# Squaring a hidden-state row on GpSimd from SBUF instead of reloading it for ScalarE: the row norms of a GRU with a mixture-of-experts stage

## The chip, the cores and the metric

The kernel runs on one core of a Trainium2 chip. The metric is the device time of one execution, in microseconds (us). The time before is the median of three runs. The profile is one further execution, recorded by the hardware profiler.

## The reference, cut to what matters

A GRU runs over 256 time steps for 16 batch rows with 512 features. Its hidden states, 4096 tokens of 512 features, then pass a mixture of eight low-rank experts of which each token uses two. The router divides a token by its norm before it multiplies by `router_w`, so every token needs the sum of its squared features.

```python
def cell(h, x):
    gi = x @ W_ih + b_ih
    gh = h @ W_hh + b_hh
    i_r, i_z, i_n = jnp.split(gi, 3, axis=-1)
    h_r, h_z, h_n = jnp.split(gh, 3, axis=-1)
    r = jax.nn.sigmoid(i_r + h_r)
    z = jax.nn.sigmoid(i_z + h_z)
    n = jnp.tanh(i_n + r * h_n)
    h_new = (1.0 - z) * n + z * h
    return (h_new, h_new)

norm = jnp.maximum(jnp.linalg.norm(x, axis=-1, keepdims=True), 1e-12)
router_logits = x / norm @ router_w
routing_weights = jax.nn.softmax(router_logits.astype(jnp.float32), axis=-1)
rw, selected_experts = jax.lax.top_k(routing_weights, TOP_K)
rw = rw / jnp.sum(rw, axis=-1, keepdims=True)
combine = jnp.sum(jax.nn.one_hot(selected_experts, N_EXPERTS, dtype=rw.dtype) * rw[..., None], axis=1)
for e in range(N_EXPERTS):
    out = out + combine[:, e, None] * (x @ Wa[e] @ Wb[e])
x = x + out
```

Everything is float32.

## The kernel before

The steps of the recurrence are written out one by one, in 32 blocks of eight (`TS = 8`); in this text t is a step's place in its block, 0 to 7. A step (`step`) has a fixed chain. PE multiplies the transposed hidden state by the recurrent weights, 16 matmuls for the r and n gates (`into_rn`, L921), then 16 for the z gate (`into_z`, L931). ACT takes the tanh for r (L947), z (L952) and n (L956). DVE forms the candidate in two instructions that read PSUM (L954, L955), then `zh` (L959), `m` (L961) and `rows` (L963), which each read two tensors in SBUF, and transposes the result into `hist` (L966). That last transpose releases the next step's matmuls. A second transpose (`back`, L974) makes the next step's row form of h.

Behind this chain the program places other work. PE multiplies the next steps' inputs (`gate_in`, L269 and L277) after each step's own matmuls. Agents bring the rest: `Early` prepares some inputs' products ahead, `Route` routes the tokens of one block, `Chunk` sorts routed tokens into expert slots in DRAM, `Slab` runs one expert on 128 slots, `Combine` gathers the two results of a token and adds them, and `Moe` handles the last three blocks without sorting. The first 29 blocks go by the sorted way, in chunks of 7, 11, 7 and 4 blocks. Every agent has a list of `Piece`s, each with a least distance in steps (`gap`), a planned matmul cost and the room in buffers that it takes. `choose` picks pieces for each step; `advance(0, ...)` issues their matmuls after the step's own, and `advance(1, ...)` issues the rest behind the step's chain. The order on every engine is then fixed by `keep_order`: each engine executes strictly in the order in which the program was written.

GpSimd (POOL) has this work in the loop: copies of a slab's weights (`wag` L677 and `wbg` L681), which wait for an earlier slab's matmuls to free a buffer; the `Early` bias additions (L391 to L393); the square root of a norm (L629, a power of one half); small operations of the top-2 (L307, L637); and the indirect DMAs that scatter tokens (L558) and gather results (L750).

A block's `Route` starts in the block after it. In t = 0 `keep` writes the 128 rows of h to DRAM (`H`, eight DMAs, L604), since the scatter needs them there. In t = 1 PE computes the router's logits from `hist` (L341), `fetch` issues a DMA on SP's queue that reads the rows back as `ht`, 128 tokens by 512 features (L612), and DVE transposes the logits (L622). In t = 3 `norm` squares `ht` on ACT with a running sum (L627), and POOL takes the root. In t = 4 and t = 5 follow the softmax and the top-2. The chunk itself reads the rows once more, as `ht2` (L552), when it scatters them; that stays as it is. The DMA list of the page counts both reloads under `ht<-H`, 58 in all, 29 of each.

Of the kernel before, what the change touches and what calls it, by code (L numbers as in the profile page):

```python
# [8 lines left out]
FP = mybir.dt.float32  # L9
# [7 lines left out]
AF = mybir.ActivationFunctionType  # L17
ALU = mybir.AluOpType
# [3 lines left out]
P = 128  # L22
TS = 8
# [21 lines left out]
def gru_moe_kernel(  # L45
# [47 lines left out]
    pe, dve, act, pool, sp = nc.tensor, nc.vector, nc.scalar, nc.gpsimd, nc.sync  # L93
    B, T, D = x.shape
    E, _, R = wa.shape
    NJ = D // P
    NQ = P // 32
# [18 lines left out]
    moe = ctx.enter_context(tc.tile_pool(name="moe", bufs=2))  # L116
# [29 lines left out]
    for side, src in enumerate((b_ih, b_hh)):  # L146
        for g in (0, 2, 1):
            tag = ("xg", "wbg")[side]
# [22 lines left out]
    ones = const.tile([P, 1], FP, name="ones")  # L171
    pool.memset(ones, 1.0)
    half = const.tile([P, 1], FP, name="half")
# [37 lines left out]
    rt = ps_r.tile([P, 512], FP, name="rt")  # L211
    pe.matmul(rt, lhsT=zero[:, 0:P], rhs=zero, start=True, stop=True)
    banks = []
    for n in range(2):
        pair = []
        for what in ("rn", "z"):
            g = ps_g.tile([P, 512], FP, name=f"{what}_{n}")
            for j in range(NJ):
                pe.matmul(
                    g[32 * j : 32 * j + 32, :], lhsT=zero[:, 0:32], rhs=zero,  # L220
                    start=True, stop=True,
# [5 lines left out]
    for n, parts in enumerate((((0, 0), (1, 0)), ((1, 2),), ((0, 2),), ((0, 1), (1, 1)))):  # L227
        for k, (side, g) in enumerate(parts):
            for j in range(NJ):
                pe.matmul(  # L230
                    bias_ps[32 * j : 32 * j + 32, n * P : (n + 1) * P],
                    lhsT=ones_sq[0:1, 0:32],
                    rhs=b_rows[side, g][:, j * P : (j + 1) * P],
                    start=(k == 0), stop=(k == len(parts) - 1),
# [102 lines left out]
    def router(h):  # L337

        for q in range(NQ):
            for c in range(NJ):  # L340
                pe.matmul(  # L341
                    rt[32 * c : 32 * c + E, 0:32].rearrange("p (b t) -> p b t", t=TS),
                    lhsT=wr_sb[:, q, :], rhs=tokens(h, q, c),
                    start=(q == 0), stop=(q == NQ - 1),
                )

    class Early:
# [57 lines left out]
        def plan(self):  # L405
            pieces = [
                Piece(then=[("load",)], takes="early"),
                Piece(gap=2, then=[("turn",)], takes="at"),
            ] + [
                Piece(gap=0, cost=c, pe=[("into", what, q)])  # L410
                for what, c in (("rn", 0.43), ("z", 0.22))
                for q in range(NQ)
            ] + [Piece(then=[("store",)], gives="early")]
            pieces[2].gap, pieces[2].takes = 1, ["ps"]
            pieces[9].then, pieces[9].gives = [("keep",)], ["ps", "at"]
            return pieces
# [19 lines left out]
    class Chunk:  # L436
# [113 lines left out]
        def fetch(self, k):  # L550
            ht = moe.tile([P, D], FP, tag="ht2", bufs=2, name=f"ht2_{self.c}_{k}")
            sp.dma_start(ht, self.rows[k].rearrange("b t d -> (b t) d"))  # L552
            self.ht = getattr(self, "ht", {})
            self.ht[k] = ht
# [37 lines left out]
    class Route:  # L592
# [14 lines left out]
                    )  # L607
            self.chunk.rows.append(hd)

        def fetch(self):  # L610
            self.ht = moe.tile([P, D], FP, tag="ht", name=f"ht_{self.i}")
            sp.dma_start(  # L612
                self.ht, self.chunk.rows[self.k].rearrange("b t d -> (b t) d")
            )

        def logits(self):
            router(self.hist)

        def soft0(self):

            self.lg = moe.tile([P, 32], FP, tag="lgs", name=f"lg_{self.i}")
            dve.transpose(self.lg, rt[:, 0:32])  # L622

        def norm(self):
            i = self.i
            ss = moe.tile([P, 1], FP, tag="ss", name=f"ss_{i}")
            act.activation(self.ht, self.ht, AF.Square, accum_out=ss)  # L627
            self.nrm = moe.tile([P, 1], FP, tag="nrm", name=f"nrm_{i}")
            pool.tensor_tensor(self.nrm, ss, half, ALU.pow)  # L629

        def soft1(self):
            self.ex, self.sm = softmax(self.i, self.lg, self.nrm)
# [5 lines left out]

        def plan(self):
            return [  # L640
                Piece(then=[("keep",)]),
                Piece(cost=0.35, pe=[("logits",)], then=[("fetch",), ("soft0",)]),
                Piece(gap=2, then=[("norm",)]),
                Piece(then=[("soft1",)]),
                Piece(then=[("soft2",)]),
            ]
# [466 lines left out]
    for i in range(NB):  # L1113
        rows, rows_next = rows_next, None
        for t in range(TS):
# [8 lines left out]
            elif m + 1 < T // 2:  # L1124
                q = 0 if t % 2 == 0 else 2
# [72 lines left out]
```

## Time and profile before

| | before |
|---|---|
| median of three runs | 1357.65 us (1355.23 to 1357.68) |
| the profiled execution | 1356.92 us |
| its span, first to last instruction | 1355.1 us, granted TensorE clock 0.994 |
| PE matmul busy | 1292.5 us (95%), 30378 matmuls |
| DVE, ACT, POOL busy | 736.2 us, 392.1 us, 284.4 us |
| moved by DMA | 158.67 MB |
| reload `ht<-H`, of the two kinds together | 58 of 256 KB |

The engines run beside one another, so their busy times are not to be added. A busy PE is a PE with a matmul in its pipeline; it is not a PE without room. Where in the step an engine's work falls is told by the timeline, which lists instructions in order of time with the idle time before each and what ended it.

### The profile page before, as it was taken

How to read it: one execution, taken by the hardware profiler on the slowest of the kernel's cores; microseconds unless marked ns; L12 is line 12 of the kernel's file. 1: busy time of each engine (PE TensorE's matmuls, PEld its weight loads, DVE VectorE, ACT ScalarE, POOL GpSimd, SP SyncE). 2: the span in 40 equal slices, each digit the busy share in tenths (PEclk: the TensorE clock that was granted, in tenths of full speed). 3: DMA queues.
4: the chain of work that ended last, by engine and by line, in shares of the span. 5: the costliest groups of instructions: out<-in, count | busy, mean ns of one | idle time of the engine just before them, and what ended most of it. 6: DMA issues, size and time to landing. Idle time of an engine off the chain costs nothing. (4 is left out here: it accounts for less than half of the span.)

```text
span 1355.1 us, 68450 instructions
## 1 busy us (share of the span) xinstructions
PE 1292.5 (95%) x30378; PEld 929.7 (69%) x30378; DVE 736.2 (54%) x2678; ACT 392.1 (29%) x1354; POOL 284.4 (21%) x504
## 2 busy tenths in 40 slices
PE   6899999999999999999999999999998999989996
PEld 3577777776677777777776677777766787768752
DVE  1455555555455555555555456555565555665543
ACT  1223222322233333233332233333332333323220
POOL 2000000102221000000003323221133033353452
PEclk8999999999999999999999999999999999999998
DMA  8532322223322111122124535553345345664685
GB/s 200 143 122 97 99 91 90 91 61 130 95 72 61 55 56 56 41 59 57 50 65 132 182 90 158 151 148 101 95 142 167 103 135 168 174 199 129 199 253 167
DMA packets 149477, 158.67 MB, mean 117 GB/s; under 512 B 22646, under 2 KB 103606, under 8 KB 149180
## 3 DMA queue, kind: packets, MB, share of 16 engines
q1 hardware_dynamic: 139760, 123.83, 31.1%
q0 software_dynamic: 9280, 30.42, 7.1%
q8 instruction: 238, 3.90, 1.2%
q14 instruction: 59, 0.48, 0.1%
q10 hardware_dynamic: 140, 0.05, 0.0%
HBM read 84.21 MB, written 69.99 MB: 114 GB/s over the span
## 5 line engine op out<-in xcount | busy, mean ns | idle before, releaser
L921 PE MATMUL rn<-whh,hist 128*32 128x256 f32 x8160 | 507.8, 381 | 19.9 <-DVE hist L966 14.1
L921 PEld LDWEIGHTS rn<-whh,hist 128*32 128x32 f32 x8160 | 264.0, 109 | 198.5 <-DVE hist L966 48.3
L269 PE MATMUL rn<-wih,xT 128*32 128x256 f32 x3712 | 307.3, 382 | 9.3 <-DMA wih<-in_L_cond_W_ih_dram 5.5
L931 PE MATMUL z<-whh,hist 128*32 128x128 f32 x8160 | 289.9, 273 | 6.4 <-issue 5.8
L954 DVE SCALAR_TENSOR_TENSOR n<-r,rn 128x128 f32<-128x128 f32 x256 | 73.5, 287 | 397.6 <-ACT r L947 393.0
L931 PEld LDWEIGHTS z<-whh,hist 128*32 128x32 f32 x8160 | 247.3, 110 | 51.7 <-issue 13.5
L277 PE MATMUL z<-wih,xT 128*32 128x128 f32 x3712 | 209.0, 274 | 5.5 <-ACT z L952 3.3
L947 ACT ACTIVATE r<-rn 128x128 f32<-128x128 f32 x256 | 70.9, 277 | 460.7 <-PE rn L921 448.8
L277 PEld LDWEIGHTS z<-wih,xT 128*32 128x32 f32 x3712 | 138.5, 110 | 77.3 <-issue 6.3
L269 PEld LDWEIGHTS rn<-wih,xT 128*32 128x32 f32 x3712 | 126.7, 110 | 19.0 <-issue 13.1
L959 DVE SCALAR_TENSOR_TENSOR zh<-z,h 128x128 f32<-128x128 f32 x255 | 77.8, 305 | 86.0 <-ACT z L952 83.1
L952 ACT ACTIVATE z<-z 128x128 f32<-128x128 f32 x256 | 71.0, 277 | 170.7 <-PE z L931 144.7
L698 PE MATMUL at_ps<-xgT,wag 128*32 128x128 f32 x2752 | 110.1, 273 | 3.9 <-issue 3.5
L629 POOL TENSOR_TENSOR nrm<-ss,half 128x1 f32<-128x1 f32 x29 | 16.2, 559 | 435.5 <-ACT ht L627 408.2
L713 PE MATMUL y_ps<-wbg,at 128*32 128x256 f32 x1376 | 103.2, 380 | 1.0 <-issue 0.9
L698 PEld LDWEIGHTS at_ps<-xgT,wag 128*32 128x32 f32 x2752 | 87.6, 110 | 13.9 <-issue 10.2
L966 DVE STREAM_TRANSPOSE hist<-rows 128x128 f32<-128x128 f32 x256 | 79.7, 311 | 8.7
L974 DVE STREAM_TRANSPOSE h<-hist 128x128 f32<-128x128 f32 x256 | 79.7, 311 | 8.7
L681 POOL COPY wbg<-wb_sb 128x512 f32 x86 | 56.3, 655 | 126.0 <-PE y_ps L713 125.9
L963 DVE SCALAR_TENSOR_TENSOR rows<-zh,m 128x128 f32<-128x128 f32 x256 | 75.9, 297 | 8.9
L721 ACT COPY y<-y_ps 128x512 f32<-128x512 f32 x86 | 50.1, 583 | 101.9 <-PE y_ps L713 88.3
L961 DVE SCALAR_TENSOR_TENSOR m<-z,n 128x128 f32<-128x128 f32 x256 | 77.7, 303 | 2.4 <-ACT n L956 1.4
(136 smaller groups left out, 1072.4 us busy)
## 6 DMA issues: line engine op xcount, KB each, us to landing
xg<-x_slots SPq DMA_DIRECT2D x344, 64.0 KB
y_slots<-y SPq DMA_DIRECT2D x86, 256.0 KB
ht<-H SPq DMA_DIRECT2D x58, 256.0 KB
x_slots<-zero SPq DMA_DIRECT2D x50, 256.0 KB
x<-in_x_dram SPq DMA_DIRECT2D x256, 32.0 KB
xr<-in_x_dram SPq DMA_DIRECT2D x32, 256.0 KB
out_dram<-xr SPq DMA_DIRECT2D x32, 256.0 KB
H<-rows SPq DMA_DIRECT2D x232, 32.0 KB
```

Of the source, the lines that this page charges most:

```text
L269: pe.matmul(rn[32 * j : 32 * j + 32, 0 : 3 * P].rearrange("p (g d) -> p g d", g=3)[:, 0:3:2, :], lhsT=xts[m][:, q, :], rhs=w[:, 0:3:2, j, ...
L277: ins = pe.matmul(zb[32 * j : 32 * j + 32, 0:P], lhsT=xts[m][:, q, :], rhs=w[:, 1, j, :], start=False, stop=(q == NQ - 1), skip_group_chec ...
L698: pe.matmul(self.ps[c32, 0:P], lhsT=self.wa[:, q, c32], rhs=self.xt[:, q, :], start=(q == 0), stop=(q == NQ - 1),)
L713: pe.matmul(self.ps[c32, half], lhsT=self.at[:, c32], rhs=self.wb[:, half], start=True, stop=True,)
L921: pe.matmul(rn[32 * j : 32 * j + 32, 0 : 2 * P].rearrange("p (g d) -> p g d", g=2), lhsT=hT[:, q, :], rhs=w(q, j)[:, 0:3:2, :], start=Fals ...
L931: pe.matmul(zb[32 * j : 32 * j + 32, 0:P], lhsT=hT[:, q, :], rhs=w(q, j)[:, 1, :], start=False, stop=(q == NQ - 1), skip_group_check=True,)
L954: dve.scalar_tensor_tensor(n, r, 1.0, rn[:, P : 2 * P], ALU.add, ALU.mult)
L959: dve.scalar_tensor_tensor(zh, z, 1.0, hrow, ALU.add, ALU.mult)
L961: dve.scalar_tensor_tensor(m, z, 1.0, n, ALU.subtract, ALU.mult)
L963: dve.scalar_tensor_tensor(hn, zh, 0.5, m, ALU.mult, ALU.subtract)
L966: dve.transpose(hist[:, t, :, lo : lo + 32], hn.rearrange("p (q c) -> p q c", q=NQ))
L974: dve.transpose(hrow.rearrange("p (q c) -> p q c", q=NQ), hT)
```

## The change

The norm no longer comes from reloaded rows. `fetch` and `norm` are gone from `Route`, and with them the DMA of the rows back into SBUF and ACT's squaring pass. In t = 0, with `keep`, a new `square` works on `hist` itself, which has the features on the partitions: POOL squares it quarter by quarter into a tile `sq` of 128 by 512, reading `hist` with a step so that the tokens come out in order, and adds the quarters up in two more instructions, to 128 by 128. In t = 3 four small matmuls with a column of ones (`sums`) add `sq` over the partitions into columns 32 to 63 of the router's PSUM bank. One DVE transpose of 64 columns then brings logits and sums together; it stands in t = 3 where the transpose of 32 columns stood in t = 1. POOL's root follows it. `sq` uses the two buffers that `ht` had.

```diff
-        def fetch(self):
-            self.ht = moe.tile([P, D], FP, tag="ht", name=f"ht_{self.i}")
-            sp.dma_start(
-                self.ht, self.chunk.rows[self.k].rearrange("b t d -> (b t) d")
-            )
+        def square(self):
+
+            sq = moe.tile([P, NQ, P], FP, tag="ht", name=f"sq_{self.i}")
+            for q in range(NQ):
+                h = self.hist[:, :, q, 16:32].rearrange("p t b -> p b t")
+                pool.tensor_mul(
+                    sq[:, q, :].rearrange("p (b t) -> p b t", t=TS), h, h
+                )
+            pool.tensor_add(sq[:, 0:2, :], sq[:, 0:2, :], sq[:, 2:4, :])
+            pool.tensor_add(sq[:, 0, :], sq[:, 0, :], sq[:, 1, :])
+            self.sq = sq
...
+        def sums(self):
+            for c in range(NJ):
+                pe.matmul(
+                    rt[32 * c : 32 * c + 1, 32:64],
+                    lhsT=ones, rhs=self.sq[:, 0, 32 * c : 32 * c + 32],
+                    start=True, stop=True,
+                )
+
         def soft0(self):
-            self.lg = moe.tile([P, 32], FP, tag="lgs", name=f"lg_{self.i}")
-            dve.transpose(self.lg, rt[:, 0:32])
-
-        def norm(self):
             i = self.i
-            ss = moe.tile([P, 1], FP, tag="ss", name=f"ss_{i}")
-            act.activation(self.ht, self.ht, AF.Square, accum_out=ss)
+            lg = moe.tile([P, 2, 32], FP, tag="lgs", name=f"lg_{i}")
+            dve.transpose(lg.rearrange("p n e -> p (n e)"), rt[:, 0:64])
+            self.lg = lg[:, 0, :]
             self.nrm = moe.tile([P, 1], FP, tag="nrm", name=f"nrm_{i}")
-            pool.tensor_tensor(self.nrm, ss, half, ALU.pow)
+            pool.tensor_tensor(self.nrm, lg[:, 1, 0:1], half, ALU.pow)
...
         def plan(self):
             return [
-                Piece(then=[("keep",)]),
-                Piece(cost=0.35, pe=[("logits",)], then=[("fetch",), ("soft0",)]),
-                Piece(gap=2, then=[("norm",)]),
+                Piece(then=[("keep",), ("square",)]),
+                Piece(cost=0.35, pe=[("logits",)]),
+                Piece(gap=2, cost=0.06, pe=[("sums",)], then=[("soft0",)]),
                 Piece(then=[("soft1",)]),
                 Piece(then=[("soft2",)]),
             ]
```

In the order of the built programs, nothing else moves: on PE 29 groups of four matmuls are added, on ACT 29 squarings go, on DVE 29 transposes stand two steps later, on SP 29 loads go, and on POOL 29 groups of six instructions are added.

## The prediction

> **What bounds the kernel now.** I read the page first, for what each engine does, then the timeline of single steps, then the groups of instructions with shapes kept apart, for durations. The chain that ended last tells of the final 17 us alone, and says nothing of the loop that the change touches.
>
> ```profile
> PE 1292.5 (95%) x30378; PEld 929.7 (69%) x30378; DVE 736.2 (54%) x2678; ACT 392.1 (29%) x1354; POOL 284.4 (21%) x504
> POOL 2000000102221000000003323221133033353452
> ```
>
> PE looks full, but the timeline says otherwise. A quiet step (t = 0 of block 13), DVE's rows with those of the released PE:
>
> ```profile
> 506.18 0.31 DVE L966 STREAM_TRANSPOSE hist<-rows 128x128 f32<-128x128 f32 x1
> 508.86 0.29 DVE L954 SCALAR_TENSOR_TENSOR n<-r,rn 128x128 f32<-128x128 f32 x1 [2.02 <-ACT r L947]
> 509.18 0.29 DVE L955 SCALAR_TENSOR_TENSOR n<-n,rn 128x128 f32<-128x128 f32 x1
> 509.73 0.29 DVE L959 SCALAR_TENSOR_TENSOR zh<-z,h 128x128 f32<-128x128 f32 x1 [0.27 <-ACT z L952]
> 509.94 0.28 DVE L961 SCALAR_TENSOR_TENSOR m<-z,n 128x128 f32<-128x128 f32 x1
> 510.26 0.29 DVE L963 SCALAR_TENSOR_TENSOR rows<-zh,m 128x128 f32<-128x128 f32 x1
> 510.59 0.31 DVE L966 STREAM_TRANSPOSE hist<-rows 128x128 f32<-128x128 f32 x1
> 510.95 0.15 PEld L921 LDWEIGHTS rn<-whh,hist 128*32 128x32 f32 x7 [0.35 <-DVE hist L966]
> ```
>
> From one hist to the next (506.49 to 510.90) is 4.41 us, and the last row shows PE's weight load idle for 0.35 us until hist came. Most steps of the loop take this 4.41, to 0.01: the step is a chain in latency, with PE's other work fitted behind it. From the timeline: 33.8 us before the first hist, 255 steps of 4.41 (1124), 111 us by which steps are longer, and 83 us after the last hist. Of the 111, 70 are pauses of PE within a step, nearly all where indirect or large DMAs run (blocks 8, 19 to 23, 26 to 31); 30 are steps where PE's filler ends after hist, from block 18 on mostly. So a piece of work costs time if it delays zh, m, rows or hist, or fills PE beyond the slack.
>
> Now a step into which POOL works:
>
> ```profile
> 499.96 0.61 POOL L677 COPY wag<-wa_sb 128x512 f32 x1 [0.75 <-PE rn L921]
> 500.51 0.29 DVE L959 SCALAR_TENSOR_TENSOR zh<-z,h 128x128 f32<-128x128 f32 x1 [0.27 <-ACT z L952]
> 500.51 0.76 POOL L681 COPY wbg<-wb_sb 128x512 f32 x1
> 500.72 0.70 DVE L961 SCALAR_TENSOR_TENSOR m<-z,n 128x128 f32<-128x128 f32 x1
> 501.45 0.29 DVE L963 SCALAR_TENSOR_TENSOR rows<-zh,m 128x128 f32<-128x128 f32 x1
> ```
>
> m takes 0.70 instead of 0.28, and ends 0.14 after POOL's copy; the step is 0.41 longer. POOL's copy in turn took 0.76 instead of 0.61, after zh. In the timeline, zh, m or rows took over 0.38 us 29 times; in 27 of them a POOL copy ran beside it, and it ended 0.14 to 0.17 after that copy's end. L954 and L955, which read PSUM, and the transposes keep their durations beside POOL copies (0.29 and 0.31). So DVE instructions with two inputs in SBUF and POOL's instructions exclude each other, one at a time.
>
> **The change part by part.**
>
> ```profile
> L392 POOL TENSOR_TENSOR ge<-ge,bias 128x128 f32<-128x128 f32 x12 | 5.5, 458 | 78.1 <-ACT ge L389 77.8
> L393 POOL TENSOR_TENSOR ge<-ge,bias 128x256 f32<-128x256 f32 x12 | 8.8, 732 | 0.0
> L787 POOL COPY hc<-hist 128x128 f32<-128x128 f32 x12 | 5.5, 496 | 4.0 <-PE a_ps L833 4.0
> L391 POOL COPY ge<-bias 128x128 f32<-128x128 f32 x12 | 3.5, 292 | 0.0
> L792 POOL TENSOR_TENSOR sq<-hc 128x512 f32<-128x512 f32 x3 | 3.2, 1059 | 2.4 <-issue 2.2
> L627 ACT ACTIVATE ht<-ht 128x512 f32<-128x512 f32 x29 | 18.0, 621 | 0.0
> L803 PE MATMUL rt<-sq,ones 128*1 128x32 f32 x96 | 2.2, 192 | 1.0 <-issue 1.0
> ```
>
> *Removed on ACT.* 29 squarings and their reads of the sum, 0.62 and 0.19 us (18.0 + 5.5 us). They follow n's tanh in t = 3, and ACT then has some 2.3 us until the next r is ready; with the two seed copies (0.77) they fit. L627 never waited for its load (0.0). Cover: the next step's 16 matmuls. I count 0; were some on the path, at most a few tenths in the blocks with several evictions, 2 us together.
>
> *Removed on SP's queue and the DMA engines.* 29 loads of 256 KB, 7.6 of 158.67 MB, or 4.8%. The load stands on SP behind the eight stores of H and waits for them (27.3 us in 26 waits, at most 3.0); behind it are clears, x loads and slab loads, all needed steps later. What may gain are the PE pauses: 4.8% of 70 us is 3.4. Most of them stand by the scatters and gathers, whose number is unchanged, so I take 1.5 (0 to 3.4).
>
> *Added on PE.* 116 matmuls at 2.2/96 = 23 ns each, 2.7 us, in t = 3. The idle time of weight loads before rn in t = 4 is 0.11 us or more in every block by the timeline, and four of these need 0.09. I take 0.5 (0 to 2.7). The wait that they bring: PE may stall for `sq`, with the whole step behind it. `sq` is issued three steps before; see the rivals.
>
> *Moved on DVE.* The transpose: 64 columns take 0.24 (L813) for 0.21, 0.9 us in sum, behind hist in t = 3 where DVE idles 2 us for r; 0. The root follows it and begins some 0.9 us later than before, still a step ahead of the softmax; the Early additions or weight copies behind it on POOL end before zh (they moved from 0.4-1.9 to 1.3-2.8 after hist). 0.
>
> *Added on POOL.* 29 times four multiplications and two additions. The additions have rows: 0.73 (L393) and 0.46 (L392), and each waits for the one before (L792 began 0.09 after its copies). The multiplication has none: 128 columns, both inputs the same tensor read with a step. From below: 0.40, by L792's (1.04 undisturbed, 1.67 ns a column over the 0.18 that is left at zero columns by L392 and L393). From above: 0.69, L392 plus twice the 0.11 by which an undisturbed stepped copy (L787, 0.40) exceeds a plain one (L391, 0.29). The Trainium skill (GPSIMD Engine Reference, 3.1 Elementwise) gives a two-input instruction about 2.6 cycles an element[...], which would be 0.46 here as in L392[...]. I take 0.61: L792's 0.40 with that term twice. The copies overlap by 0.06 at their joints, so from hist's end: 0.1 + 4 x 0.55 + 0.06 = 2.4 after the multiplications, 3.2 after the first addition, 3.7 after the second. zh begins at 3.24, m at 3.45, rows at 3.77 (above: 509.73, 509.94, 510.26 less 506.49). By the skill's 0.46 all would end at 3.1, ahead of zh, and the sum would be about 5 us instead of 11.
>
> With 0.61 the second addition meets zh or m: zh waits for 3.73 and ends 0.14 later, 0.34 late; or zh goes first, and the addition holds m until 3.85, 0.25 late. 0.3 a block. Behind it comes whatever POOL has queued. I took the place of each square in the changed order, and the times before of the instructions around it:
> - Blocks 1 to 7, 9, 13, 14, 18, 27: nothing that holds much is ready. 12 x 0.3 = 3.6.
> - Blocks 10 to 12, 15 to 17, 21 to 25, 28, 29: a `wag` copy, in about half with its `wbg`, is ready. Many ran 4 us before hist, when POOL was ahead of the loop; now they queue behind the squares and run through zh, m and rows. The trace's such meetings cost 0.41 (500.72 above) to 0.70. 13 x 0.6 = 7.8, less 1.6 where PE's filler was late in that step anyway (0.05 to 0.65 us in the last seven) = 6.2.
> - Blocks 8, 19, 20, 26: scatters ahead of or behind the squares; 4 x 0.3 = 1.2. The scatters shift by up to 4 us, with over 5 us to the slabs' first loads.
>
> Sum: 11.0 + 0.5 - 1.5 = +10.0. On the profiled execution's 1356.92 this is 1366.9; the median of the runs is 0.73 above that execution, so the median would be about 1367.6. I say 1367. With multiplications of 0.40 it is +3, with 0.69 +16.
>
> **The rivals.**
> - *The squares end in time and the lighter DMA load decides (not slower).* At 0.46 or less the squares are past before zh. This needs them to end by about 3.2 after hist. Then only doubled weight copies meet the chain (3 to 5 us), and what PE pauses less (3.4) and ACT gives back (2) can cancel or outweigh it: 1353 to 1358. For it: L792's 1.67 ns. Against: L787's step.
> - *Heavier meetings.* Multiplications of 0.7 or longer, or DVE's turns delaying POOL so that zh, m and rows each meet one: 0.6 alone and 0.9 with copies, 12 x 0.6 + 13 x 0.9 + 4 x 0.6 - 2 = 19: 1375.
> - *PE waits for the squares.* POOL in order behind scatters would hold `sums`. Against: by the times before, POOL's preceding instruction has ended before hist in 26 of the 29 blocks, and 3.65 after it at worst (block 8); squares are done by some 8, and `sums` comes at 16. If it happened in the three scatter stretches, some 3 us each on top: 1376.
> - *The change does not do what it says.* The built order shows it, and no other piece moves; under 1 in 100.
>
> **How the numbers follow.** Runs of this kernel can tell 0.2% (2.7 us) from no change. The main case has 0.58, heavier meetings 0.20, PE waiting 0.03; the first rival 0.19, of which 0.09 within 0.2% and 0.10 below. Of the main case's light end 0.01 falls within 0.2%. So faster 0.10, same 0.10, slower 0.80. The range for 8 in 10: from 1356, the light end with the rival's upper half, to 1377, the heavy case with 2 us of changed PE pauses.
>
> **What would show it.** In the profile after: POOL's squares start 0.1 after the block's last hist and take 3.6 in all; means of zh, m and rows rise, by some 0.3 us in t = 0 of each block and nowhere else; t = 0 is 4.7 to 5.0 long in blocks 1 to 7, and t = 1 to 7 keep 4.41. No PE row waits on sq for more than 0.1. ACT's r does not start earlier in t = 4. I am wrong if the steps t = 0 keep 4.41 in blocks 1 to 7 (multiplications shorter than 0.5), if PE waits on POOL in t = 3, or if the loss or gain lies in blocks 19 to 31 alone with PE pauses of another length.

## The result, and the profile after

The changed kernel takes 1368.35 us (median of six runs, 1366.37 to 1370.96); the kernel before took 1356.81 us beside it (six runs, 1355.23 to 1357.68). The ratio is 1.0079, with a 95% interval of 1.0067 to 1.0091: slower by 11.5 us. The forecast was 1367. The profiled execution of the changed kernel took 1370.96 us, 2.6 above its median, with a span of 1369.2 us; its granted clock was 0.990, for 0.994 before.

The page of the changed kernel, engines and POOL's 40 slices:

```profile
PE 1295.9 (95%) x30610; PEld 933.4 (68%) x30610; DVE 748.1 (55%) x2678; ACT 375.3 (27%) x1296; POOL 365.3 (27%) x678
POOL 2011111113331111111113414332234135263462
```

POOL's busy time grew by 80.9 us and the span by 14. Its groups, with shapes kept apart, show the new work, and in the last row the root:

```profile
L615 POOL TENSOR_TENSOR sq<-hist 128x128 f32<-128x128 f32 x116 | 46.7, 436 | 181.6 <-DVE hist L978 181.6
L618 POOL TENSOR_TENSOR sq<-sq 128x256 f32<-128x256 f32 x29 | 21.2, 730 | 2.3
L619 POOL TENSOR_TENSOR sq<-sq 128x128 f32<-128x128 f32 x29 | 13.4, 461 | 2.3
L641 POOL TENSOR_TENSOR nrm<-lg,half 128x1 f32<-128x1 f32 x29 | 16.6, 573 | 344.1 <-DVE lg L638 344.1
```

The additions are as forecast (0.73 and 0.46). The multiplication is not: 0.436 us, where the forecast took 0.61. What that does is seen in a t = 0 in which nothing else waits on POOL, the timeline of block 13 (POOL's rows, then four of DVE's):

```profile
510.35 1.57 POOL L615 TENSOR_TENSOR sq<-hist 128x128 f32<-128x128 f32 x4 [5.30 <-DVE hist L978]
512.00 0.73 POOL L618 TENSOR_TENSOR sq<-sq 128x256 f32<-128x256 f32 x1
512.81 0.47 POOL L619 TENSOR_TENSOR sq<-sq 128x128 f32<-128x128 f32 x1
...
509.95 0.31 DVE L978 STREAM_TRANSPOSE hist<-rows 128x128 f32<-128x128 f32 x1
513.51 0.29 DVE L971 SCALAR_TENSOR_TENSOR zh<-z,h 128x128 f32<-128x128 f32 x1 [0.26 <-ACT z L964]
513.72 0.28 DVE L973 SCALAR_TENSOR_TENSOR m<-z,n 128x128 f32<-128x128 f32 x1
514.36 0.31 DVE L978 STREAM_TRANSPOSE hist<-rows 128x128 f32<-128x128 f32 x1
```

From hist's end (510.26) the four squares take to 511.92, and the last addition ends at 513.28, 3.02 after hist. zh begins at 513.51, 3.25 after hist, and keeps its 0.29. The step is 4.41 long: the squares are past in time. In block 15 they are too, but something is queued behind them:

```profile
580.86 1.56 POOL L615 TENSOR_TENSOR sq<-hist 128x128 f32<-128x128 f32 x4 [7.02 <-DVE hist L978]
583.30 0.46 POOL L619 TENSOR_TENSOR sq<-sq 128x128 f32<-128x128 f32 x1
583.98 0.61 POOL L689 COPY wag<-wa_sb 128x512 f32 x1 [0.22 <-issue]
584.53 0.68 POOL L693 COPY wbg<-wb_sb 128x512 f32 x1
...
584.01 0.72 DVE L971 SCALAR_TENSOR_TENSOR zh<-z,h 128x128 f32<-128x128 f32 x1 [0.26 <-ACT z L964]
584.66 0.69 DVE L973 SCALAR_TENSOR_TENSOR m<-z,n 128x128 f32<-128x128 f32 x1
585.38 0.29 DVE L975 SCALAR_TENSOR_TENSOR rows<-zh,m 128x128 f32<-128x128 f32 x1
585.71 0.31 DVE L978 STREAM_TRANSPOSE hist<-rows 128x128 f32<-128x128 f32 x1
```

The additions end at 583.76, and the weight copies that stood behind them start 0.22 later: at 3.2 after hist, just when zh starts. zh takes 0.72 and m 0.69, each ending 0.13 to 0.14 after a copy; the step (580.77 to 586.02) is 5.25 long, 0.84 too much.

Where all of the time went was worked out step by step from the timelines, against the quiet step of 4.41. "Chain" is what steps have too much between the start of n's tanh and hist's end, where zh, m and rows stand; "other" is all else in a step (PE's filler that ends late, and PE's pauses). Columns t0 to t6 are the chain's excess in the steps with t = 0, 1, 4 and 6; the other steps change little. The first two rows are the two profiled executions above; the others belong to the experiments, where kernels of one letter (e1 to e4, r with e5, s) ran on one chip.

| profiled execution | t0 | t1 | t4 | t6 | chain, all | other | span |
|---|---|---|---|---|---|---|---|
| before | 0.3 | 0.5 | 0.3 | 6.4 | 9.2 | 102.0 | 1355.1 |
| after | 9.4 | 1.6 | 2.1 | 4.9 | 19.9 | 106.5 | 1369.2 |
| r_before | 0.3 | 0.5 | 0.2 | 6.0 | 8.3 | 107.2 | 1359.1 |
| r_after | 9.0 | 1.5 | 2.0 | 4.9 | 18.7 | 112.1 | 1377.4 |
| r_gate | 3.4 | 2.3 | 1.8 | 4.7 | 13.6 | 116.8 | 1375.6 |
| e5_act_dve | 0.2 | 0.5 | 2.3 | 5.8 | 10.5 | 106.4 | 1362.1 |
| s_before | 0.3 | 0.5 | 0.2 | 6.1 | 8.6 | 106.1 | 1357.9 |
| s_after | 9.1 | 1.5 | 2.2 | 5.4 | 19.7 | 105.6 | 1370.2 |
| s_no_squares | 0.3 | 0.5 | 2.4 | 6.1 | 10.6 | 104.8 | 1359.5 |
| s_act_dve | 1.3 | 0.6 | 1.8 | 5.9 | 10.9 | 104.9 | 1361.7 |
| e1_no_squares | 1.7 | 1.6 | 2.2 | 5.4 | 11.6 | 38.1 | 1292.8 |
| e2_squares_added | 10.1 | 5.7 | 1.0 | 3.6 | 21.0 | 44.4 | 1308.1 |
| e3_gate | 5.6 | 3.6 | 1.6 | 3.7 | 15.9 | 37.2 | 1296.3 |
| e4_longer | 17.2 | 5.6 | 1.6 | 3.8 | 28.7 | 37.3 | 1310.1 |

On three chips the change adds 10.7, 10.4 and 11.1 us to the chain, most of it in t = 0 (9.1, 8.7, 8.8). "Other" changes by +4.5, +4.9 and -0.5: that part does not repeat. What lies before the first hist and after the last is in neither column; it changes by -1.1, +2.3 and +1.7 us.

### The profile page after: what moved, and what is told of

It is laid out like the page before. It is cut to its first block, busy times and chain, and to the rows that moved or that the text cites. A ratio compares the mean times of both kernels' runs of the same rounds, so it can differ in the third digit from the quotient of the medians.

```text
span 1369.2 us, 68820 instructions
## 1 busy us (share of the span) xinstructions
PE 1295.9 (95%) x30610; PEld 933.4 (68%) x30610; DVE 748.1 (55%) x2678; ACT 375.3 (27%) x1296; POOL 365.3 (27%) x678
## 3 DMA queue, kind: packets, MB, share of 16 engines
q1 hardware_dynamic: 135584, 116.23, 28.7%
## 4 chain that ended last, share of the span: by engine, by line
PE 86%; DVE 6%; DMA 3%; issue 2%; ACT 1%; another core or an unknown queue 1%; SPq 0%; ACTq 0%; DVEq 0%
PE rn L933 34%; PE z L943 17%; PE rn L269 13%; PE z L277 6%; PE y_ps L725 5%; PE at_ps L710 5%; PE a_ps L845 1%; PE gi L377 1%; DVE zh L971 1%; DVE rows L975 1%; DVE m L973 1%; PE rt L341 1%; DMA whh<-in_L_cond_W_hh_dram 1%; PE o_ps L882 1%; DVE hist L978 1%
## 5 line engine op out<-in xcount | busy, mean ns | idle before, releaser
L269 PE MATMUL rn<-wih,xT 128*32 128x256 f32 x3712 | 304.0, 383 | 11.6 <-DMA wih<-in_L_cond_W_ih_dram 8.2
L943 PE MATMUL z<-whh,hist 128*32 128x128 f32 x8160 | 286.5, 273 | 5.7 <-issue 5.2
L277 PE MATMUL z<-wih,xT 128*32 128x128 f32 x3712 | 206.0, 275 | 4.8 <-issue 2.4
L971 DVE SCALAR_TENSOR_TENSOR zh<-z,h 128x128 f32<-128x128 f32 x255 | 84.2, 330 | 88.2 <-ACT z L964 85.2
L641 POOL TENSOR_TENSOR nrm<-lg,half 128x1 f32<-128x1 f32 x29 | 16.6, 573 | 344.1 <-DVE lg L638 344.1
L615 POOL TENSOR_TENSOR sq<-hist 128x128 f32<-128x128 f32 x116 | 46.7, 436 | 181.6 <-DVE hist L978 181.6
```

Source lines behind the costliest of these rows:

```text
L269: pe.matmul(rn[32 * j : 32 * j + 32, 0 : 3 * P].rearrange("p (g d) -> p g d", g=3)[:, 0:3:2, :], lhsT=xts[m][:, q, :], rhs=w[:, 0:3:2, j, ...
L277: ins = pe.matmul(zb[32 * j : 32 * j + 32, 0:P], lhsT=xts[m][:, q, :], rhs=w[:, 1, j, :], start=False, stop=(q == NQ - 1), skip_group_chec ...
L943: pe.matmul(zb[32 * j : 32 * j + 32, 0:P], lhsT=hT[:, q, :], rhs=w(q, j)[:, 1, :], start=False, stop=(q == NQ - 1), skip_group_check=True,)
L971: dve.scalar_tensor_tensor(zh, z, 1.0, hrow, ALU.add, ALU.mult)
```

## The experiments

Chips differ here: the kernel before takes 1301.44 us on the chip of e1 to e4, 1361.3 on that of r and e5, 1358.54 on that of s. So a kernel is compared by its ratio to the kernel before on its own chip (95% interval in brackets), and the microseconds in the expectations of e1 to e4, which were written for a chip like the first, hold only as differences.

**Without the squares.** The changed kernel, with the multiplications and additions left out and the sums fed from a tile of ones. What remains of the change is all the rest: no reload, no square on ACT, the new matmuls, the wider transpose, the later root.

```diff
         def square(self):
-            sq = moe.tile([P, NQ, P], FP, tag="ht", name=f"sq_{self.i}")
...
-            self.sq = sq
+            pass
...
-                    lhsT=ones, rhs=self.sq[:, 0, 32 * c : 32 * c + 32],
+                    lhsT=ones, rhs=ones_sq[:, 32 * c : 32 * c + 32],
```

> The changed kernel with GpSimd's squares and additions left out; the four small matmuls of each block read a constant tile instead (so the norms are those of a constant). All else is as in the changed kernel: no reload, no ScalarE squaring, the matmuls, the transpose in t = 3. Theory (the loss is what GpSimd's squares do to the chain in t = 0): 1355 to 1358, at or a little below the kernel before, since only the gain of the removed reload and squaring is left. Rival (the matmuls, the moved transpose or the later root cost it): 1364 or more.

1295.03 us, ratio 0.9958 [0.9945, 0.9971]: 6.4 us faster than before. That is on the theory's side, and more than the small gain that it had allowed for.

**The squares alone.** The kernel before, which keeps its reload and ACT's square, with the six POOL instructions added in t = 0; nothing reads their result.

```diff
-                Piece(then=[("keep",)]),
+                Piece(then=[("keep",), ("square",)]),
```

> The kernel before with the six GpSimd instructions added in t = 0 into a tile that nothing reads; the reload and ScalarE's squaring stay. Theory: the whole loss, plus the small gain of the removals that is missing here: 1367 to 1371. Rival (the loss needs the new matmuls or the removed load): under 1362.

1309.25 us, 1.0059 [1.0045, 1.0073]. The squares alone make the kernel slower by 7.8 us, between what the theory and the rival had said. t = 0 has 10.1 us of chain delay without any other part of the change, for 1.7 in e1_no_squares, which has every other part. So the loss is the squares'. That the same kernel without reload gains 6.4 while this one loses only 7.8 leaves a question on the removals, to which this trace has the answer (below).

**Holding back what follows the squares.** The changed kernel, with a copy of one column of the *next* hist behind the additions: POOL cannot go on to a weight copy before the step's chain is over.

```diff
             pool.tensor_add(sq[:, 0, :], sq[:, 0, :], sq[:, 1, :])
+            gate = moe.tile([P, 1], FP, tag="gate", name=f"gate_{self.i}")
+            pool.tensor_copy(gate, hists[(self.i + 1) % 3][:, 0, 0, 16:17])
```

> The changed kernel with one GpSimd copy of one column behind each block's additions, which reads the next step's hist and so keeps GpSimd's following weight copies back until the chain of t = 0 is over. Theory (the squares themselves end at 3.0 us, before zh; the weight copies held back behind them hit zh, m and rows): the nine or ten blocks with a copy in t = 0 lose their 0.4 to 0.9 us, 1361 to 1364. Rival (the squares themselves slow the chain, wherever they lie): 1367 to 1370, unchanged. Second rival (copies held back longer make PE wait for weights): above 1370.

1297.33 us, 0.9974 [0.9960, 0.9988]: faster than before on this chip, 2.3 us above e1_no_squares. The changed kernel itself was not run on this chip, so what the gate gains there over it is not measured. By blocks, the delays in t = 0 tell the explanations apart. With the gate the blocks with a weight copy behind the squares (10 to 12, 15 to 17, 21 to 25, 28, 29) have 0.00 us together; in the changed kernel they have 5.6 to 5.8, and in e2_squares_added, on this chip, 4.9. What remains is mostly in blocks 8, 19 and 26, where scatters stand ahead of the squares: 4.2 us here, 2.3 to 2.6 in the changed kernel.

**Longer squares.** The changed kernel with one more addition of 256 columns behind the others, so that POOL's work ends 0.55 later.

```diff
             pool.tensor_add(sq[:, 0, :], sq[:, 0, :], sq[:, 1, :])
+            pool.tensor_add(sq[:, 2:4, :], sq[:, 2:4, :], sq[:, 2:4, :])
```

> The changed kernel with one more addition of 128 by 256 behind the others, read by nothing, so that GpSimd's work of t = 0 ends at 3.8 us after hist instead of 3.0, behind the start of zh at 3.24. Theory (what decides is whether it ends before zh): the eleven blocks that lost nothing now lose 0.3 to 0.6 us each, and those with weight copies somewhat more than before: 1372 to 1378. Rival (a cost by the length of GpSimd's work, 29 x 3.0 us for some 10 us): 0.8 us more of it a block, 1370 to 1371.

1308.46 us, 1.0053 [1.0038, 1.0069]; t = 0 now has 17.2 us of delay. This is close to the case that the prediction had taken for the real one. Its timeline in block 13:

```profile
506.54 0.46 POOL L619 TENSOR_TENSOR sq<-sq 128x128 f32<-128x128 f32 x1
506.95 0.62 POOL L620 TENSOR_TENSOR sq<-sq 128x256 f32<-128x256 f32 x1
...
507.25 0.47 DVE L972 SCALAR_TENSOR_TENSOR zh<-z,h 128x128 f32<-128x128 f32 x1 [0.26 <-ACT z L965]
507.64 0.28 DVE L974 SCALAR_TENSOR_TENSOR m<-z,n 128x128 f32<-128x128 f32 x1
```

The added instruction ends at 507.57, and zh, held by it, at 507.72. The blocks with no weight copy behind the squares, which cost nothing in the changed kernel (block 4 apart), cost 0.17 to 0.35 each here, and 0.56 in block 27. That is less than this run's expectation (0.3 to 0.6), and about the 0.3 that the prediction had put on such a meeting; the changed kernel's squares are just too short for it.

**The same on a second chip.** To see what depends on the chip, before, after and the gate ran once more, with a new version, e5_act_dve: the squares on ACT (which loses a square in t = 3 anyway), the additions on DVE behind the logits in t = 1, POOL left with the root alone. Its edit stands below, behind the gate's rows.

> The kernel before once more, for its trace on the chip of these runs. The runs of e1 to e4 had the kernel before at 1301 us instead of 1357, and their traces have pauses of TensorE within a step of some 7 to 15 us where the earlier trace had 70. If the chip makes that difference, this trace has the short pauses too and the kernel before takes about 1301; if the chip is the earlier one, 1357. Ratio 1.000 in both cases.

1361.49 us, 1.0005 [0.9993, 1.0018].

> The changed kernel once more, beside the others on one chip. Theory (two opposed terms: what e1 gained by the removed reload and squaring, -6.4, and what the squares cost the chain, +7.8 in e2): ratio 1.000 to 1.003 where the pauses are short. Rival (the loss of 11.5 us is the same everywhere): 1.008. On the earlier chip: 1.008 again.

1374.94 us, 1.0100 [1.0084, 1.0116]: a little more than the 1.008 expected for a chip like the first.

> The gate kernel once more, on the same chip as the changed kernel. Theory (weight copies held back behind the squares make most of the chain's loss): 4 to 7 us below the changed kernel. Rival (the squares themselves): no difference to it.

1376.66 us, 1.0115 [1.0098, 1.0132]. A miss: the gate gains nothing over the changed kernel here. It does its work, as its block 15 shows:

```profile
584.35 0.47 POOL L619 TENSOR_TENSOR sq<-sq 128x128 f32<-128x128 f32 x1
586.29 0.19 POOL L622 COPY gate<-hist 128x1 f32<-128x1 f32 x1 [1.47 <-DVE hist L980]
586.98 0.62 POOL L691 COPY wag<-wa_sb 128x512 f32 x1 [0.50 <-issue]
...
585.06 0.29 DVE L973 SCALAR_TENSOR_TENSOR zh<-z,h 128x128 f32<-128x128 f32 x1 [0.26 <-ACT z L966]
585.27 0.28 DVE L975 SCALAR_TENSOR_TENSOR m<-z,n 128x128 f32<-128x128 f32 x1
```

zh and m are back at 0.29 and 0.28, wag comes after hist, and t = 0 has 3.4 us of delay for 9.0. But "other" is 116.8 for 112.1: the chain gives 5.1 us and the rest takes 4.7. Why PE pauses more is not settled. It is not a wait for the held-back weights, the second rival of e3_gate: no row of PE's waits names `wag` or `wbg`. Block 21 alone has 8.0 us for 4.5, most of the growth in t = 1 and t = 2 (3.9 for 0.4). There the gate holds back two gathers too: they start 2.1 us after hist, in the changed kernel 0.7 before it. That this brings the pauses is likely, not shown. On the chip of the first experiments, where pauses are short, e3_gate has no more of them than its partners (37.2 us of "other").

```diff
-                pool.tensor_mul(
+                act.activation(
                     self.sq[:, q, :].rearrange("p (b t) -> p b t", t=TS),
...
-                Piece(cost=0.35, pe=[("logits",)]),
+                Piece(cost=0.35, pe=[("logits",)], then=[("fold",)]),
```

> The changed kernel with the squares on ScalarE (four instructions of 128 by 128 reading hist, behind n's tanh in t = 0) and the two additions on VectorE in t = 1, behind the second transpose, where it idles for r; GpSimd has only the root. Theory (ScalarE and VectorE have room there, and GpSimd's squares were the only cost of the change): as e1, 0.4 to 0.6% below the kernel before on a chip with short pauses, and below it by up to 0.3% on the earlier chip. Rival (four more ScalarE instructions ahead of r, or VectorE's additions against GpSimd's copies, delay the chain): ratio 1.000 or more.

1366.0 us, 1.0039 [1.0025, 1.0053], and t = 0 and t = 1 are those of before. Off POOL the squares cost nothing in the chain (ACT's 116 take 425 ns each, DVE's two additions 0.39 and 0.30), yet the kernel is slower than before by 4.7 us, where the theory had it faster: a miss. The rival's ratio came, but not for its reason, a delay by these instructions. Of the 4.7 the chain shows 2.1, in t = 4 (2.3 for 0.2); the rest is open.

**And on a third.** Before, after, no squares and the version on ACT and DVE, side by side.

> The kernel before again, as the partner of the next three on one chip. Where its time is near 1301 its pauses of TensorE in the scatter blocks 8, 19, 20, 26 and 30 should be some 7 to 12 us in sum as in e1 to e4, where it is near 1360 some 50. Ratio 1.000.

1358.28 us, 0.9994 [0.9976, 1.0012].

> The changed kernel. The delay of zh, m and rows in t = 0, summed over all blocks, was 9.4 and 8.9 us in its two traces and 0.3 in both of the kernel before. Theory: this term does not depend on the chip, 9 us again. On a chip like that of e1 to e4 the ratio is e1's gain of 6.4 less these 9: 1.001 to 1.004; on one like the first, 1.008 to 1.010. Rival (the gain of e1 is the squares' POOL time itself, and there is no gain from the removals): 1.006 or more on both.

1372.37 us, 1.0096 [1.0074, 1.0118]: as expected for a chip like the first.

> The changed kernel without GpSimd's squares and additions (the matmuls read a constant; the norms are those of a constant). On a chip like that of e1: 0.9958 again. On a chip with the long pauses: theory (only the squares cost, but the removals gain nothing there, as with ScalarE's squares in e5): 1.000 to 1.004, against 1.008 to 1.010 for the changed kernel. Rival (the removals gain everywhere): 0.997 or less.

1361.42 us, 1.0018 [1.0002, 1.0033]: the theory's range for long pauses.

> The squares on ScalarE and the additions on VectorE in t = 1, GpSimd left with the root. On a chip with long pauses: 1.004 again. On a chip like that of e1 to e4: theory (nothing of it touches the chain, as e5's trace had 0.2 us of delays in t = 0): near the kernel without squares, 0.995 to 0.998, below both kernels. Rival: 1.000 or more, as on the chip of e5.

1362.07 us, 1.0022 [1.0010, 1.0034]: again slower than before, by less than in e5_act_dve.

On one chip, then: the squares on POOL cost 10.9 us (1372.37 less 1361.42), of which the chain shows 9.1; all the rest of the change costs 2.9, where the first experiment's chip had shown a gain of 6.4. The 2.0 us by which s_no_squares' chain exceeds s_before's lie in t = 4 (2.4 for 0.2). Block 9 shows them. Before, with POOL's rows; t = 3's hist ends at 379.95:

```profile
379.64 0.57 POOL L629 TENSOR_TENSOR nrm<-ss,half 128x1 f32<-128x1 f32 x1 [2.30 <-DVE rows L963]
380.59 0.61 POOL L677 COPY wag<-wa_sb 128x512 f32 x1 [0.39 <-issue]
```

After; t = 3's hist ends at 382.06:

```profile
382.62 0.57 POOL L641 TENSOR_TENSOR nrm<-lg,half 128x1 f32<-128x1 f32 x1 [3.17 <-DVE lg L638]
383.57 0.61 POOL L689 COPY wag<-wa_sb 128x512 f32 x1 [0.38 <-issue]
...
385.23 0.61 POOL L693 COPY wbg<-wb_sb 128x512 f32 x1
...
385.30 0.68 DVE L971 SCALAR_TENSOR_TENSOR zh<-z,h 128x128 f32<-128x128 f32 x1 [0.27 <-ACT z L964]
```

The root waits for the transposed sums and starts 0.56 after hist instead of 0.31 before it. Four copies of slab weights stand behind it; now the last of them meets zh. In the changed kernel seven blocks (9, 21, 22, 24, 26, 27, 29) have such a meeting in t = 4, in the kernel before one. That the later root brings them is read from the order on POOL: in blocks 21, 22 and 26, too, all that stands behind the root starts 0.8 to 1.1 later after hist than before.

**What the removals are worth.** In e2_squares_added, which still reloads, the timelines of SP's queue, ACT and PE in block 20:

```profile
769.77 0.59 SPq L604 DMA_DIRECT2D H<-rows  x1
772.69 0.33 SPq L623 DMA_DIRECT2D ht<-H  x1
...
775.37 0.63 ACT L638 ACTIVATE ht<-ht 128x512 f32<-128x512 f32 x1 [5.81 <-DMA ht<-H]
776.47 0.48 ACT L249 COPY rn<-bias 128x384 f32<-128x384 f32 x1
...
777.00 1.08 PE L269 MATMUL rn<-wih,xT 128*32 128x256 f32 x8 [3.58 <-ACT rn L249]
```

The reload, whose place in the program is t = 1, was issued in t = 4, behind the eight stores of H, which stand on SP behind loads that wait for scatters. ACT waited 5.81 us for it with the next step's seeds and r behind it, and PE stood for 3.58. This step is 8.87 us long. In this kernel ACT waits 8.1 us for the reload in sum (three blocks); in the three traces of before it waits 0.0. It is also what "other" shows: 44.4 us here, 37.2 to 38.1 in the three kernels of the same chip that have no reload. There the loop runs 55 us faster, and a load that is hidden on the slower chips is late. The squares are not what makes it late: in e1_no_squares, which has none, SP issues the last of block 20's stores of H until 18.3 us after the hist at the start of t = 0 (19.0 in e2_squares_added, 7.4 in the kernel before on the first chip), when t = 3 has already begun, at 13.2. No trace of the kernel before was taken on that chip; that its own reload is late there is inferred from these two kernels and from the gain of e1_no_squares.

## Why the prediction was right, point by point

The number came out (1367 for 1368.35), and the working did not in several of its terms. The mechanism was right: POOL's new work makes zh and m wait in t = 0. But by the prediction's own sign of being wrong, t = 0 of 4.41 in blocks 1 to 7 (it is 4.41 in all of them but block 4), its main term, the squares' own meeting, failed, and the sum came out by luck.

- **The multiplication's duration.** Forecast 0.61, from L792 with L787's step counted twice; measured 0.436. The surcharge for the step was the error: that a copy with a step takes 0.11 more (L787) does not carry over to this multiplication. The estimate from the two-input rate of the Trainium skill (GPSIMD Engine Reference, 3.1 Elementwise), 0.46, was right within 0.03. The squares end 3.0 after hist, not 3.7.
- **The blocks in which only the squares run.** Forecast 12 x 0.3 = 3.6 us; measured 0.74 to 0.77, all in block 4, where the `Early` bias instructions ran ahead of the squares and the last addition ended 4.66 after hist. e4_longer has 3.8 in the same blocks: the price of a meeting was right, its occurrence wrong.
- **The blocks with weight copies behind.** Forecast 7.8, less 1.6 for steps late anyway = 6.2; measured 5.8, 5.6 and 5.6 on three chips, and 0.00 with the gate. This step was right, for its reason.
- **The scatter blocks 8, 19, 20, 26.** Forecast 1.2; measured 2.6, 2.3 and 2.6, nothing of it in block 20. In the other three the squares, behind scatters, start about 3.6 after hist, and meet more of zh, m and rows than an addition's tail.
- **The later root.** Forecast 0 ("end before zh"); measured 1.6 to 2.2 in t = 4, with or without squares on POOL. The copies behind the root take 0.56 each of POOL's time; with four queued, as in block 9, the last ends 3.8 after hist. Beside it, t = 1 grew by 1.0 and t = 6 shrank by 0.7 to 1.5, as copies moved past the squares (e5_act_dve has neither).
- **The removals.** Forecast -1.5; "other" went by +4.5, +4.9 and -0.5, and by -1.3, -0.8 and -1.2 where POOL has no squares (s_no_squares, e5_act_dve, s_act_dve). No gain beyond that can be told on these chips; on the chip of e1 to e4 it is some 6 to 7 us, as inferred above, by a wait that the prediction counted out because it was 0.0 in its trace.
- **Added on PE.** 7.3 us of busy PE for the 2.7 forecast, as each of these float32 matmuls stands as two records (232 for 116, 31 ns each). It is hidden: in t = 4 PE begins behind hist without delay, 0.0 in sum, before and after.

The sum in its own terms: 0.8 + 5.7 + 2.5 in t = 0, 1.9 in t = 4, +1.0 and -1.1 in t = 1 and t = 6, is 10.8 of the chain, beside the forecast's 11.0 from t = 0 alone. Two misses, the squares' own meeting (-2.8) and the root with the scatters (+3.2), cancelled; nothing in the prediction gave a reason for that. Of the rivals the first was half right: the squares do end in time, but the copies cost 5.7 where it gave them 3 to 5, and it had neither scatters nor root. PE never waited for the squares: no row of its waits names them. One sum of the prediction is short: the first hist ends at 38.2 us, not 33.8, so that its division of the span adds up to 1352 of 1355. No term rests on it.

What stays open is the growth of "other" in two of the three pairs. Block 19 grew in all three (12.4 to 18.0, 14.7 to 17.4 and 13.4 to 17.0 us), in part without any squares (15.0 in s_no_squares).

## What to carry to other kernels

On an engine that is idle in sum, ask not only whether a new instruction fits, but what stands behind it in its queue: here six instructions passed in time and let two weight copies go at the worst moment. Where two engines exclude each other, a window of 3.2 us that the new work fills to 3.0 is full, and moving the work to engines outside the exclusion (ACT, and DVE in a step where it idles) kept t = 0 as it was, though it brought no gain either: the kernel was still 0.2 to 0.4% slower than before. A load that never waited in one trace has a margin, not a proof: on a chip where the kernel ran 4% faster the same load, in e2_squares_added, held ACT for 5.8 us.

## What the runs showed that was not expected

A POOL multiplication of 128 columns, both operands the same strided tensor, took 0.436 us, no more than a contiguous addition of 128 columns (0.461).

The same kernel differed by 66 us between two chips at nearly the same clock, and the difference lies in what the table calls "other" (104.8 and 38.1 us). The page's line of the cores, s_no_squares and e1_no_squares:

```profile
core 0: 1359.5 us, clock 0.992
```

```profile
core 0: 1292.8 us, clock 0.990
```

Block 19, t = 4, in ACT's and POOL's timelines, for s_no_squares with PE's last z matmul and two rows of its weight loads:

```profile
746.29 0.28 ACT L951 ACTIVATE r<-rn 128x128 f32<-128x128 f32 x1 [1.06 <-PE rn L925]
750.79 0.28 ACT L956 ACTIVATE z<-z 128x128 f32<-128x128 f32 x1 [4.22 <-remote]
...
746.41 0.27 PE L935 MATMUL z<-whh,hist 128*32 128x128 f32 x1
747.00 0.16 PEld L269 LDWEIGHTS rn<-wih,xT 128*32 128x32 f32 x4 [0.55 <-issue]
748.47 0.15 PEld L277 LDWEIGHTS z<-wih,xT 128*32 128x32 f32 x4 [0.57 <-issue]
...
746.32 0.98 POOL L558 DMA_INDIRECT x_slots<-ht,ilo  x1 [0.30 <-issue]
747.60 0.97 POOL L558 DMA_INDIRECT x_slots<-ht,ihi  x1 [0.31 <-issue]
748.87 0.97 POOL L558 DMA_INDIRECT x_slots<-ht,ilo  x1 [0.30 <-issue]
```

e1_no_squares:

```profile
731.24 0.28 ACT L951 ACTIVATE r<-rn 128x128 f32<-128x128 f32 x1 [0.47 <-PE rn L925]
732.12 0.28 ACT L956 ACTIVATE z<-z 128x128 f32<-128x128 f32 x1 [0.59 <-PE z L935]
...
730.52 1.03 POOL L558 DMA_INDIRECT x_slots<-ht,ihi  x1 [0.20 <-issue]
731.86 0.97 POOL L558 DMA_INDIRECT x_slots<-ht,ilo  x1 [0.30 <-issue]
```

While POOL issues scatters, ACT's tanh for z comes after an idle time of 4.22 us on the one chip and of 0.59 on the other; POOL's rows for the indirect DMAs take the same 0.97 to 1.03 on both. On the long one the profile does not put the end of the wait down to PE's z ("remote"): the last z matmul stands there as ended at 746.68, 4.1 us before, though a matmul's end is modelled. In that time PE itself is held. Its weight loads come about four at a time with 0.55 to 0.61 us of idle time between, and for these the profile shows no wait ("issue"). On the other chip the eight loads of a gate follow one another in 0.24 to 0.34 us. In r_gate's block 21 they come two at a time, 0.49 to 0.60 apart, while POOL issues gathers. What makes these pauses, and why they are long on one chip, was not found.
